# Counting neighbours: two halves of a row packed into one number, one running count over 512 columns instead of 1024

## The chip, the cores and the metric

The kernel runs on one core of a Trainium2 chip. The metric is the device time in microseconds (us) of one execution. Engines are named as in the profile: PE is TensorE (matmul), PEld its weight loads, DVE is VectorE, ACT is ScalarE, POOL is GpSimd, SP the engine whose queue issues most DMAs.

## The reference, cut to what matters

Four graph layers over 16 graphs of 1024 nodes with 64 features. The change touches the first layer, which drops some edges and then takes quantiles over the neighbours that are left:

```python
neigh = (adj_ > 0) & ~eye
ni = neigh.astype(jnp.int32)
rank = jnp.cumsum(ni, axis=-1) - ni          # neighbours left of this column
nb = ni.sum(-1)
skip = jnp.where(nb > T, (nb + K - 1) // K, 1)
rem = neigh & (sk > 1) & (rank % sk == sk - 1) & mask[:, :, None]
rem = rem | jnp.swapaxes(rem, 1, 2)
adj_d = jnp.where(rem, 0.0, adj_)
vals = jnp.where(adj_d[..., None] > 0, x[:, None, :, :], jnp.inf)
s = jnp.sort(vals, axis=2)                   # three quantiles of it, per node and feature
```

The kernel needs the running count along each row of 1024 columns, for 16 x 1024 rows. An edge is in about 6% of the places.

## The kernel before, in words

Graphs are handled in eight pairs. For each pair there are four pieces of work.

- **Sort** (`sort_begin`, `sort_pair`): the 2 x 64 feature columns of a pair are sorted over the nodes, on DVE. A forward pass of 55 compare steps (lines 772 to 776) writes which pairs swapped to DRAM (`m_d`, in groups of four steps). A backward pass (lines 804 to 814) reads those back and turns them into a code per node (`code`), which is transposed (lines 848 to 854), stored to `y_d`, and read by `weights`. At three steps of the forward pass the part that the sort gives up is checked: `tensor_reduce` (line 780) writes `rest_`, a tile with two buffers, and line 784 takes the maximum of the column `past` and `rest_`.
- **Neighbours** (`neighbours`, lines 859 to 958): for each of two graphs, in two halves of four row tiles. A row tile `a` of the adjacency is loaded, `ni` becomes its 0/1 form in 8 bits (line 874), GpSimd clears the diagonal (line 875), and a scan on DVE counts along 1024 columns (line 879, `cum`, 16-bit floats). PE transposes `a` through the two PSUM banks of the pool `nbp` (tile `pk`). Then small operations on four columns (`sk`, lines 894 to 904) find the skip of each row, three ACT passes over `cum` mark the removed edges (`rem`, lines 908 to 910), and PE and ACT build `ndT`, the matrix that is left.
- **Select** (`weights`, `select`, `compact`): the quantiles, by matmuls of `ndT` with `wt` (lines 975 and 1097) and bit work on DVE. `compact` (lines 1227 to 1300) ends with the 56 matmuls of line 1288; it too raises `past` (line 1253).
- **Extras and layers** (`extras`, `layers`): nodes that need a second look, then the rest of the four layers, with the rows `adjT` read from DRAM. The attention of the last layer runs lines 1564 to 1579 for each row tile; line 1586 is the last sum before the output is stored.

`past` is a column of "did any shortcut fail" marks. Where it ends above zero, a general version of the kernel runs at the end. It is one buffer in place, so its updates run in the order in which the program states them.

The order in the program is this: select of pair `p`, extras and layers of pair `p`, then `prepare(p + 1)` (the neighbours of the next pair), then `sort_pair(p + 1)`, then `sort_begin(p + 2)`. A scheduler orders the instructions of each engine from that when the program is built, by readiness and priority, and keeps every data dependency of the stated order. The order on each engine is then fixed; each engine runs its instructions in it. For the first pair the sort is stated before the neighbours.

```python
made = prepare(pr + 1, nb, nbp)
sort_pair(pr + 1, cur, sop)
...
rest_ = so.tile([P, 1], F32, name="rest_", bufs=2)
nc.vector.tensor_reduce(rest_, ...)
nc.vector.tensor_max(past, past, rest_)
```

Of the kernel before, what the change touches and what calls it, by code (L numbers as in the profile page):

```python
# [9 lines left out]
F32 = mybir.dt.float32  # L10
BF16 = mybir.dt.bfloat16
I32 = mybir.dt.int32
U8 = mybir.dt.uint8
U16 = mybir.dt.uint16
I16 = mybir.dt.int16
F16 = mybir.dt.float16
F8 = mybir.dt.float8e5
AF = mybir.ActivationFunctionType
ALU = mybir.AluOpType
AX = mybir.AxisListType  # L20
# [3 lines left out]
P = 128  # L24
# [18 lines left out]
def gnn_stack(ctx, tc, x, adj, nodemask, w, out):  # L43
# [10 lines left out]
    nc = tc.nc  # L54
    B, N, C = x.shape
# [4 lines left out]
    const = ctx.enter_context(tc.tile_pool(name="const", bufs=1))  # L60
    dram = ctx.enter_context(tc.tile_pool(name="dram", bufs=1, space=DRAM))

    ident = const.tile([P, P], F32, name="ident")
    make_identity(nc, ident)
    ident_b = const.tile([P, P], BF16, name="ident_b")
# [83 lines left out]
    past = const.tile([P, 1], F32, name="past")  # L149
# [21 lines left out]
    with tc.tile_pool(name="io", bufs=1, side="right") as io:  # L171
        at0 = io.tile([P, P], I32, name="at0")
        nc.gpsimd.iota(at0, pattern=[[1, P]], base=0, channel_multiplier=0)
        nc.vector.tensor_copy(count, at0)
        at1 = io.tile([P, P], I32, name="at1")
        nc.gpsimd.iota(at1, pattern=[[1, P]], base=0, channel_multiplier=-1)
        nc.vector.tensor_single_scalar(below, at1, 0, op=ALU.is_gt)
    minus_b = const.tile([P, P], BF16, name="minus_b")
    nc.vector.tensor_scalar_mul(minus_b, ident, -1.0)
    taus = const.tile([P, NT, 3], F32, name="taus")  # L180
# [678 lines left out]
    def neighbours(b, ndT, row10, qb, qz, nb, nbp):  # L859

        mask = maskf[:, b * NT : (b + 1) * NT]
        HT = NT // 2
        dq, coef = row10[:, :, :3], row10[:, :, 3:9].rearrange("p t (k s) -> p t k s", s=2)
        pad = 32
        wide = nb.tile([P, NT, pad + N], F8, name="ni")
        nc.gpsimd.memset(wide[:, :, pad - 1 : pad], 0.0)
        ni = wide[:, :, pad:]
        rem = nb.tile([P, NT, N], F8, name="rem")
        for t0 in range(0, NT, HT):
            cum = nb.tile([P, HT, N], F16, name="cum")  # L870
            for t in range(t0, t0 + HT):
                a = nb.tile([P, N], F32, name="a", bufs=2)
                nc.sync.dma_start(a, adj[b, t * P : (t + 1) * P, :])
                nc.vector.tensor_single_scalar(ni[:, t, :], a, 0.0, op=ALU.is_gt, saturate=False)
                nc.gpsimd.tensor_mul(  # L875
                    ni[:, t, t * P : (t + 1) * P], ni[:, t, t * P : (t + 1) * P], offdiag, saturate=False
                )

                nc.vector.tensor_tensor_scan(  # L879
                    cum[:, t - t0, :], ni[:, t, :], wide[:, t, pad - 1 : pad - 1 + N], 0.0, op0=ALU.add, op1=ALU.add  # L880
                )
                for q in range(0, NT, 4):
                    pt = nbp.tile([P, 4, P], F32, name="pk")
                    for k in range(4):
                        nc.tensor.transpose(pt[:, k, :], a[:, (q + k) * P : (q + k + 1) * P], ident)  # L885
                    at = nb.tile([P, 4, P], F32, name="at", bufs=3)
                    nc.scalar.copy(at, pt)  # L887
                    nc.scalar.dma_start(
                        a_d[b % 4, q : q + 4, :, t * P : (t + 1) * P].rearrange("j p n -> p j n"), at
                    )  # L890


            sk = nb.tile([P, 4, HT], F32, name="sk")
            nc.vector.tensor_tensor(sk[:, 2, :], cum[:, :, N - 1], ni[:, t0 : t0 + HT, N - 1], op=ALU.add)
            nbi = nb.tile([P, HT], I32, name="nbi")
            nc.vector.tensor_scalar_add(nbi, sk[:, 2, :], 2.0)
            nc.vector.tensor_single_scalar(nbi, nbi, 2, op=ALU.logical_shift_right)
            nc.vector.tensor_single_scalar(sk[:, 0, :], sk[:, 2, :], 2 * MAX_DEGREE, op=ALU.is_gt)
            nc.vector.tensor_mul(sk[:, 0, :], sk[:, 0, :], mask[:, t0 : t0 + HT])
            nc.vector.tensor_copy(sk[:, 1, :], nbi)  # L900
            nc.vector.scalar_tensor_tensor(sk[:, 1, :], sk[:, 1, :], 1.0, sk[:, 0, :], op0=ALU.add, op1=ALU.mult)
            nc.vector.tensor_scalar(sk[:, 2, :], sk[:, 1, :], -3.0, 4.0, op0=ALU.mult, op1=ALU.add)
            nc.vector.tensor_scalar_add(sk[:, 1, :], sk[:, 1, :], -1.0)
            nc.vector.scalar_tensor_tensor(sk[:, 3, :], sk[:, 1, :], -1.0, sk[:, 1, :], op0=ALU.mult, op1=ALU.mult)
            for t in range(t0, t0 + HT):
                k = t - t0
                sq = nb.tile([P, N], F32, name="sq")
                nc.scalar.activation(sq, cum[:, k, :], AF.Square, bias=sk[:, 2, k : k + 1], scale=1.0)
                nc.scalar.activation(sq, sq, AF.Square, bias=sk[:, 3, k : k + 1], scale=1.0)
                nc.scalar.activation(rem[:, t, :], sq, AF.Relu, bias=one, scale=-1.0, saturate=False)  # L910


                for blocks, to in (
                    ([(j, t) for j in range(t + 1)], ndT[:, : t + 1, t * P : (t + 1) * P]),
                    ([(t, i) for i in range(t)], ndT[:, t, : t * P].rearrange("p (i n) -> p i n", n=P)),
                ):
                    for n, (j, i) in enumerate(blocks):
                        if n % 4 == 0:
                            pk = nbp.tile([P, 4, P], F32, name="pk")
                        terms = [  # L920
                            (ni[:, i, j * P : (j + 1) * P], ident_b),
                            (rem[:, i, j * P : (j + 1) * P], minus_b),
                            (minus_b, rem[:, j, i * P : (i + 1) * P]),
                        ]
                        if i == j:
                            terms.append((ident_b, ident_b))
                        last = n % 4 == 3 or n == len(blocks) - 1
                        for m, (lhs, rhs) in enumerate(terms):
                            nc.tensor.matmul(  # L929
                                pk[:, n % 4, :], lhs, rhs, start=(n % 4 == 0 and m == 0),  # L930
                                stop=(m == len(terms) - 1 and last),
                            )
                        if last:
                            n0, m = n - n % 4, n % 4 + 1
                            nc.scalar.activation(to[:, n0 : n + 1, :], pk[:, :m, :], AF.Relu, saturate=False)  # L935
        pn = nbp.tile([P, 4, P], F32, name="pk")[:, 0, :NT]
        for i in range(NT):
            for j in range(NT):
                nc.tensor.matmul(
                    pn[:, i : i + 1], ndT[:, j, i * P : (i + 1) * P], ones_b[:, 0:1],  # L940
                    start=(i == 0 and j == 0), stop=(i == NT - 1 and j == NT - 1),
                )
        nc.gpsimd.tensor_copy(row10[:, :, 9], ids)

        last = nb.tile([P, NT], F32, name="last")
        nc.vector.tensor_scalar_add(last, pn, -1.0)
        lasts = last.rearrange("p (t o) -> p t o", o=1).to_broadcast([P, NT, 3])
        fr = nb.tile([P, 2, NT, 3], F32, name="fr")
        fi = nb.tile([P, NT, 3], I32, name="fi")
        nc.vector.tensor_mul(fr[:, 0], lasts, taus)  # L950
        nc.vector.tensor_scalar_add(fi, fr[:, 0], -0.4)
        nc.vector.tensor_copy(fr[:, 1], fi)
        nc.vector.tensor_sub(dq, lasts, fr[:, 1])
        nc.vector.tensor_scalar(qb, dq, -2048.0, -2048.0, op0=ALU.mult, op1=ALU.add)
        nc.vector.tensor_scalar(qz, dq[:, :, 0], -1.0, 1.0, op0=ALU.mult, op1=ALU.add)
        nc.vector.tensor_sub(fr[:, 0], fr[:, 0], fr[:, 1])
        nc.vector.tensor_mul(coef[:, :, :, 1], fr[:, 0], shares)
        nc.vector.tensor_sub(coef[:, :, :, 0], shares, coef[:, :, :, 1])
# [663 lines left out]
    for pr in range(pairs):  # L1622
# [17 lines left out]
        with ExitStack() as beside:  # L1640
# [5 lines left out]
            else:  # L1646
                nb_, nbp_ = side_pools()
                nb, nbp = beside.enter_context(nb_), beside.enter_context(nbp_)
# [69 lines left out]
```

## Time and profile before

| What | Value |
|---|---|
| runs, median of 3 | 5790.94 us (5787.52 to 5797.8) |
| the profiled execution | 5786.15 us, its span 5784.4 us |
| DVE busy | 5034.9 us, 87% of the span |
| PE busy | 4378.1 us, 76% |
| ACT busy | 3789.4 us, 66% |
| scans of 1024 columns, 128 of them | 292.4 us, 2285 ns each |
| chain that ended last, by engine | PE 40%, DVE 24%, ACT 23%, DMA 9%, issue 3% |

Busy time is the time in which an engine worked; where several engines take turns, no engine is busy all the time, and the time is set by the chain of work that passes from one to the other. The kernel has eight periods. In the trace a period is cut at two events: the first `wt` of a pair (line 975), and the last matmul of line 1288. From the first to the second is called the select stage here, from the second to the first `wt` of the next pair the side stage.

### The profile page before, as it was taken

To read this page: it belongs to the slowest core of one execution; us is meant where nothing else is said; L and a number is where in the kernel's file an instruction comes from. 1 tells how busy PE (TensorE), PEld (TensorE's weight loads), DVE (VectorE), ACT (ScalarE), POOL (GpSimd) and SP (SyncE) were. 2 spreads that over 40 slices of the span, in tenths; PEclk is the share of its full clock that TensorE was granted. 3 is DMA by queue.
4 is the path that set the end of the run, shared out by engine and by line. 5 is a ranking of instruction groups with operands and counts; after the bars stand their busy time and mean duration, and the time that the engine had idled before them with its cause. 6 is when DMAs were issued, how large, how long until landed. Compare 5 with 4: busy or idle time off the path is not lost.

```text
span 5784.4 us, 114212 instructions
## 1 busy us (share of the span) xinstructions
PE 4378.1 (76%) x45010; PEld 2731.3 (47%) x45010; DVE 5034.9 (87%) x13175; ACT 3789.4 (66%) x5739; POOL 169.8 (3%) x292
## 2 busy tenths in 40 slices
PE   1488677896878958788588885788767886779956
PEld 1355443554435544455434554355543554535642
DVE  9899888998889987999879998899888998888755
ACT  2587657775586855867558666686657866477835
POOL 3000000000000000000000000000000000000000
PEclk5699878997789977899688996899878997789967
DMA  3401264013631047210562115611255012630030
GB/s 128 127 23 45 86 205 133 29 38 113 220 96 35 28 133 237 62 40 23 166 211 55 41 53 167 203 32 40 82 175 172 26 40 90 215 110 18 10 100 5
DMA packets 519811, 551.45 MB, mean 95 GB/s; under 512 B 263296, under 2 KB 413056, under 8 KB 519264
## 3 DMA queue, kind: packets, MB, share of 16 engines
q1 hardware_dynamic: 376864, 459.65, 25.5%
q10 hardware_dynamic: 140064, 81.84, 4.6%
q8 instruction: 355, 5.82, 0.4%
q0 software_dynamic: 2336, 2.57, 0.2%
q14 instruction: 192, 1.57, 0.1%
HBM read 360.17 MB, written 183.76 MB: 94 GB/s over the span
## 4 chain that ended last, share of the span: by engine, by line
PE 40%; DVE 24%; ACT 23%; DMA 9%; issue 3%; POOL 0%; SPq 0%; ACTq 0%; DVEq 0%; POOLq 0%
PE comb L1097 13%; ACT sign L1152 8%; PE cand L1197 6%; PE bank L1462 5%; DVE y L1168 4%; PE comb L1288 3%; ACT y L1105 3%; DMA adjT<-a_d 2%; DVE cum L879 2%; DMA a_d<-at 2%; DVE wt L975 2%; DVE cand L1205 2%; PE pk L929 2%; ACT nat L1128 1%; PE bank L1446 1%
## 5 line engine op out<-in xcount | busy, mean ns | idle before, releaser
L1097 PE MATMUL comb<-wt,ndT 128*128 128x512 fp8e5 x6144 | 1439.2, 386 | 144.4 <-ACT sign L1152 111.8
L1105 ACT ACTIVATE y<-comb,qb 128x512 int16<-128x512 f32 x1152 | 743.4, 712 | 505.3 <-PE comb L1097 504.2
L1097 PEld LDWEIGHTS <-ndT 128*128 128x128 fp8e5 x6144 | 591.1, 99 | 864.7 <-issue 231.6
L1152 ACT ACTIVATE sign<-comb,lower 128x1024 fp8e5<-128x1024 int16 (+1 forms) x640 | 694.5, 1085 | 0.0
L1152 ACT ACTIVATE sign<-comb,half 128x1024 fp8e5<-128x1024 int16 (+1 forms) x640 | 689.1, 1077 | 0.0
L1197 PE MATMUL cand<-vtab,sign 128*128 128x48 f16 (+1 forms) x18432 | 663.1, 191 | 23.1 <-DVE agg L1074 16.2
L1168 DVE TENSOR_TENSOR y<-y 128x512 uint16<-128x512 uint16 (+5 forms) x896 | 669.4, 789 | 10.8 <-PE comb L1150 10.0
L1197 PEld LDWEIGHTS <-sign 128*128 128x128 fp8e5 x18432 | 637.6, 96 | 82.0 <-issue 21.2
L1205 DVE COPY_PREDICATED cand<-w_f,cand 128x256 f32<-128x256 uint16 (+1 forms) x1536 | 531.9, 378 | 86.1 <-PE cand L1197 83.7
L887 ACT COPY at<-pk 128x512 f32<-128x512 f32 x256 | 147.3, 586 | 372.7 <-PE pk L885 199.8
L1150 PE MATMUL comb<-ident_b,y 128*128 128x128 bf16 x4608 | 307.2, 218 | 101.9 <-ACT sign L1152 70.8
L929 PE MATMUL pk<-minus_b,rem 128*128 128x128 bf16 x1024 | 231.9, 251 | 178.8 <-ACT rem L910 178.8
L1150 PEld LDWEIGHTS <-y 128*128 128x128 bf16 x4608 | 284.9, 97 | 127.1 <-issue 126.9
L929 PE MATMUL pk<-ident_b,ni 128*128 128x128 bf16 x1024 | 229.1, 247 | 110.4 <-ACT ndT L935 60.7
L879 DVE TENSOR_TENSOR_SCAN cum<-ni 128x1024 f16<-128x1024 fp8e5 x128 | 292.4, 2285 | 15.5 <-POOL ni L875 15.5
L885 PE MATMUL pk<-ident,a 128*128 128x128 f32 x1024 | 192.1, 330 | 149.9 <-DMA a<-in_adj_dram 100.1
L1462 PE MATMUL bank<-att,hs 128*64 128x512 f32 x512 | 191.1, 857 | 122.0 <-ACT hs L1578 122.0
L1462 PE MATMUL bank<-adjT,nd 128*64 128x512 f32 x896 | 256.2, 642 | 29.9 <-DMA adjT<-a_d 29.6
L975 DVE TENSOR_SCALAR wt<-node 128x2048 uint8<-128x2048 f16 x224 | 262.5, 1220 | 18.4 <-PE comb L1288 18.1
L775 DVE TENSOR_TENSOR s<-s 128x512 f32<-128x512 f32 (+1 forms) x440 | 276.0, 627 | 0.0
L776 DVE TENSOR_TENSOR s<-s 128x512 f32<-128x512 f32 (+1 forms) x440 | 275.1, 625 | 0.0
L1163 DVE TENSOR_SCALAR y<-y 128x4608 int16<-128x4608 int16 x128 | 173.5, 1355 | 90.7 <-ACT y L1105 89.3
(381 smaller groups left out, 8355.7 us busy)
## 6 DMA issues: line engine op xcount, KB each, us to landing
adjT<-a_d SPq DMA_DIRECT2D x336, 512.0 KB
a<-in_adj_dram SPq DMA_DIRECT2D x128, 512.0 KB
a_d<-at ACTq DMA_DIRECT2D x256, 256.0 KB
m_d<-swapped SPq DMA_DIRECT2D x104, 512.0 KB
swapped<-m_d SPq DMA_DIRECT2D x104, 512.0 KB
n_d<-nat SPq DMA_DIRECT2D x128, 128.0 KB
x_d<-xr SPq DMA_DIRECT2D x48, 256.0 KB
comb_x<-x_d ACTq DMA_DIRECT2D x24, 512.0 KB
```

Of the source, the lines that this page charges most:

```text
L775: nc.vector.tensor_tensor(to_lo, lo, hi, op=ALU.max)
L879: nc.vector.tensor_tensor_scan(cum[:, t - t0, :], ni[:, t, :], wide[:, t, pad - 1 : pad - 1 + N], 0.0, op0=ALU.add, op1=ALU.add)
L929: nc.tensor.matmul(pk[:, n % 4, :], lhs, rhs, start=(n % 4 == 0 and m == 0), stop=(m == len(terms) - 1 and last),)
L975: nc.vector.tensor_scalar(wt[g][:, :, k : k + 4, :].bitcast(U8), node, 4.0 * (25 + CODE * (8 * g + k)), 4.0 * 26, op0=ALU.add, op1=ALU.min,)
L1097: nc.tensor.matmul(pw, ndT[:, j, t * P : (t + 1) * P], wt[1 + g8][:, j].rearrange("p w c -> p (w c)"), start=(j == 0), stop=(j == NT - 1),)
L1105: nc.scalar.activation(y[:, 0, chunks, at : at + 8 * d_].rearrange("p q (w d) -> p q w d", d=d_), pw.rearrange("p (w q d) -> p q w d", w=8 ...
L1150: nc.tensor.transpose(pt[:, q - q0, :], y[:, 0, q, :].bitcast(BF16), ident_b)
L1152: nc.scalar.activation(signs[tl][s][:, q0:q1, :], pt.bitcast(I16), AF.Sign, bias=before[s], scale=-1.0, saturate=False,)
L1168: nc.vector.tensor_tensor(v[:, :, :, :n], v[:, :, :, :n], v[:, :, :, n : 2 * n], op=ALU.max)
L1197: nc.tensor.matmul(cand[:, e, at : at + 12 * d_].rearrange("p (d l) -> p d l", l=12), signs[tl][sec][:, chunk, :], tab[:, q, :, half_ * 12 ...
L1205: nc.vector.copy_predicated(v[:, :, :, dst : dst + k], mk.to_broadcast([P, 2, C // 2, k]), v[:, :, :, frm : frm + k])
L1462: nc.tensor.matmul(po[to : to + C, :], lhs, rhs[:, f * HALF : (f + 1) * HALF], start=(j == 0), stop=(j == NT - 1))
```

## The change

The scan counts both halves of a row at once. PE adds the left half of `ni` and 65536 times the right half into one PSUM bank of 512 columns (two matmuls, with the identity and `high_b` as weights), and the same right half, shifted by one column, once more (a third matmul). The shift for the left half stays with the scan's second operand. The scan then runs over 512 columns and writes 32-bit integers, which are read back as two 16-bit halves. The totals of the two halves are added, the left total is added to the start value of the right half, and the first of the three ACT passes becomes two passes over 512 columns each. Because the packed number must stay below 2^24 to be exact, the largest last count of each half of the row tiles is checked: `many` is reduced from `cum`, and `past` is raised by it. That is one more update of `past` for each half, four for each pair, stated in `neighbours`.

```diff
+    high_b = const.tile([P, P], BF16, name="high_b")
+    nc.vector.tensor_scalar_mul(high_b, ident, 65536.0)
...
         for t0 in range(0, NT, HT):
-            cum = nb.tile([P, HT, N], F16, name="cum")
+            cum = nb.tile([P, HT, N // 2], I32, name="cum")
+            halves_ = cum.bitcast(U16).rearrange("p t (n f) -> p t n f", f=2)
             for t in range(t0, t0 + HT):
...
+                both_ = nbp.tile([P, 4, P], F32, name="pk").rearrange("p k n -> p (k n)")
+                nc.tensor.matmul(both_, ident_b, ni[:, t, : N // 2], start=True, stop=False)
+                nc.tensor.matmul(both_, high_b, ni[:, t, N // 2 :], start=False, stop=False)
+                nc.tensor.matmul(both_[:, 1:], high_b, ni[:, t, N // 2 : N - 1], start=False, stop=True)
                 nc.vector.tensor_tensor_scan(
-                    cum[:, t - t0, :], ni[:, t, :], wide[:, t, pad - 1 : pad - 1 + N], 0.0, op0=ALU.add, op1=ALU.add
+                    cum[:, t - t0, :], both_, wide[:, t, pad - 1 : pad - 1 + N // 2], 0.0, op0=ALU.add, op1=ALU.add
                 )
...
-            sk = nb.tile([P, 4, HT], F32, name="sk")
-            nc.vector.tensor_tensor(sk[:, 2, :], cum[:, :, N - 1], ni[:, t0 : t0 + HT, N - 1], op=ALU.add)
+            sk = nb.tile([P, 6, HT], F32, name="sk")
+            for f in range(2):
+                nc.vector.tensor_tensor(
+                    sk[:, 4 + f, :], halves_[:, :, N // 2 - 1, f], ni[:, t0 : t0 + HT, (f + 1) * N // 2 - 1], op=ALU.add
+                )
+            nc.vector.tensor_add(sk[:, 2, :], sk[:, 4, :], sk[:, 5, :])
+            many = nb.tile([P, 1], F32, name="many")
+            nc.vector.tensor_reduce(many, cum[:, :, N // 2 - 1], axis=AX.X, op=ALU.max)
+            nc.vector.tensor_scalar_add(many, many, 1.0 - 2.0**24)
+            nc.vector.tensor_max(past, past, many)
...
             nc.vector.tensor_scalar(sk[:, 2, :], sk[:, 1, :], -3.0, 4.0, op0=ALU.mult, op1=ALU.add)
+            nc.vector.tensor_add(sk[:, 4, :], sk[:, 4, :], sk[:, 2, :])
...
-                nc.scalar.activation(sq, cum[:, k, :], AF.Square, bias=sk[:, 2, k : k + 1], scale=1.0)
+                for f in range(2):
+                    nc.scalar.activation(
+                        sq[:, f * N // 2 : (f + 1) * N // 2], halves_[:, k, :, f], AF.Square,
+                        bias=sk[:, 2 + 2 * f, k : k + 1], scale=1.0,
+                    )
```

## The prediction

> **What bounds the kernel now.** I read the engine rows first, then the stretches by stage, then the groups of the side stage, then single events of `past`.
>
> ```profile
> PE 4378.1 (76%) x45010; PEld 2731.3 (47%) x45010; DVE 5034.9 (87%) x13175; ACT 3789.4 (66%) x5739; POOL 169.8 (3%) x292
> ```
>
> DVE is busiest, but 87% is a mean over stages. The stretches, select and side stage of the second and the last period (columns: stretch, length, then busy us and count of PE, PEld, DVE, ACT, POOL, granted clock, DMA share, GB/s):
>
> ```profile
> 281.00:664.00 383.00, 332.66 (x3866) 210.84 (x3865) 361.82 (x912) 279.41 (x455) 3.12 (x4) 0.94 0.11 33
> 664.00:982.00 318.00, 216.47 (x1776) 129.06 (x1775) 265.98 (x731) 195.17 (x267) 12.93 (x24) 0.76 0.59 185
> ...
> 5170.00:5529.00 359.00, 321.65 (x3841) 206.10 (x3840) 275.71 (x740) 277.29 (x451) 2.02 (x2) 0.96 0.07 15
> 5529.00:5784.00 255.00, 150.17 (x1094) 86.27 (x1092) 133.91 (x392) 101.92 (x120) 3.20 (x6) 0.67 0.17 56
> ```
>
> The side stage takes 318 us with a next pair to prepare, and 255 us in the last period, where neither neighbours nor a sort run. So extras and layers alone need about 244 us up to their last attention (5529 to 5773), and 311 us (664 to 975) with the rest between them. DVE works 84% of that stage. What fills it:
>
> ```profile
> L879 DVE TENSOR_TENSOR_SCAN cum<-ni 128x1024 f16<-128x1024 fp8e5 x16 | 36.6, 2286 | 2.1 <-POOL ni L875 2.1
> L814 DVE TENSOR_TENSOR code<-code,xo 128x1024 uint16<-128x1024 uint16 (+1 forms) x33 | 22.2, 672 | 0.4
> L804 DVE TENSOR_TENSOR xo<-code 128x512 uint16<-128x512 uint16 (+1 forms) x54 | 21.9, 405 | 0.7
> ...
> L806 DVE TENSOR_TENSOR xo<-xo,swapped 128x512 uint16<-128x512 uint16 x39 | 16.4, 420 | 2.9 <-DMA swapped<-m_d 2.4
> ```
>
> The scans are only 36.6 us of it. The backward pass of the sort is 84.3 us (these three rows and lines 808, 811, 812 with 6.0, 9.1 and 8.7). It costs little now because it lies in the gaps of extras and layers. That cover is what the change touches, through `past`:
>
> ```profile
> 457.77 0.42 DVE L780 TENSOR_REDUCE rest__10637<-s 128x1 f32<-128x256 f32 x1
> ...
> 638.66 0.16 DVE L1253 TENSOR_TENSOR past<-past,over 128x1 f32<-128x1 f32 x1
> ...
> 644.77 0.15 DVE L784 TENSOR_TENSOR past<-past,rest__10637 128x1 f32<-128x1 f32 x1
> ...
> 645.17 0.41 DVE L780 TENSOR_REDUCE rest__10695<-s 128x1 f32<-128x256 f32 x1
> ```
>
> The sort's first check is computed at 457.77, but its update of `past` waits until 644.77, behind the second `compact` (638.66), which stands earlier in the program. The second check (506.31) takes the other buffer of `rest_`, so the third check (645.17) and all of the sort behind it wait too. Today the wait ends with the select stage.
>
> **The change, part by part.**
>
> *The scan.* The scan of 8 columns (line 1242) has a median of 174 ns, that of 1024 has 2285, so a column costs (2285 - 174) / 1016 = 2.08 ns and 512 columns 174 + 504 x 2.08 = 1.22 us: 1.06 us less, 128 times, 136 us of DVE (17 us in each of eight pairs). Its first input now comes from PSUM. The nearest rows are two sums of 128x512, line 1488 from PSUM and line 1489 from SBUF: 691 ns each, so I take nothing for that.
>
> Against that row stands the Trainium skill, Perfetto Trace Analysis, section Optimizing Scalar/DVE Operations: an access costs VectorE about 60 ns on SBUF and about 125 ns on PSUM. By that page, as an estimate, the 128 scans would give back 8 us.
>
> *Small operations.* Each half gains seven operations on four columns or one and loses one; the removed one (line 894) takes 157 ns. 32 x 6 x 0.16 = 31 us busy at most, 4 us a pair.
>
> *ACT.* Two Squares of 512 replace one of 1024 (1146 ns). Nearest rows: copies of 128x512, 586 ns (line 887), and 712 ns in line 1105. 128 x (2 x 0.59 - 1.15) = 4 us, at most 35 us by the dearer row; ACT has room (66%). Nothing on the path.
>
> *PE.* 3 x 128 matmuls of 512 columns. Line 1097 runs eight such in 1.9 us when the clock is full, 0.24 us each, mean 386 ns: 92 to 148 us, 12 to 18 in a side stage where PE idles a third of the time. The new wait is a ring: DVE (`ni`), POOL, PE (pack), DVE (scan). Queued behind the pack on PE are the eight transposes of the same row tile, and the pack holds one of the two `pk` banks until the scan has read it. In the built order other DVE work stands between `ni` and its scan. I take it as covered and leave it in the range of the stage.
>
> *The hold.* `neighbours` of the next pair is stated before `sort_pair` of that pair, and now updates `past` four times. By the mechanism just shown the sort's third check must wait for the fourth of these. I compared the order of DVE's instructions in the two built programs, which is fixed. Of the 187 operations of a backward pass, in each of the seven later sorts all 187 stand ahead of the last sum of the layers before the change. After it, one does (an early read of `code`). Rows of the changed order in the second period:
>
> ```
> 1787 last two attention products (old line 1573)
> 1789 past<-past,many              the fourth
> 1793 past<-past,rest__10855       the sort's first check
> 1798 rest__10913                  its third check
> 1801 sort goes on (25 forward operations left)
> 1811 last sum of the layers (old line 1586)
> 1831 backward pass begins, 186 operations
> 2049 first wt of the next pair
> ```
>
> So DVE does the rest of the sort when extras, layers and neighbours are done, and the next select waits, since `wt` needs the code. The tail from the last attention to the first `wt`: 25 forward operations 15 us (lines 772, 775, 776: 5.5 + 4.4 + 5.1 in this stage); from the last forward operation through the store and reload of `swapped` to line 806 5 us (147.9 to 152.8 in the first stage); the backward pass 84 us busy, 90 us with the gaps of a dependent chain (a step of 0.44 + 0.43 + 0.70 takes 1.65, 261.99 to 263.64); differences and quantile constants that stand between 6 us. `last` stands early in the backward pass and needs the whole end of the neighbours on ACT and PE. That took 24 to 28 us after `sk` was ready (754.88 to 778.62, 148.97 to 176.48), and only about 20 us of DVE work stand between: 5 us. SP's queue now has the 24 `vtab` loads, up to 10 in a row at 0.6 to 0.9 us each, between the reloads of `swapped`, of which one serves 6.6 us of steps: 5 us. From the last backward operation to `wt`, 11 us:
>
> ```profile
> 270.42 1.06 ACT s L848
> ...
> 275.08 2.94 DMA y_d<-s
> 278.04 2.59 DMA node<-y_d
> ...
> 281.38 13.73 DVE wt L975 x12
> ```
>
> Sum 15 + 5 + 90 + 6 + 5 + 5 + 11 = 137; I take 135, where some 7 us are there now (975 to 982). Bounds: 120 if the waits hide each other, 150 if they don't.
>
> What comes back: without the sort the stage up to the last attention is shorter than 311 us, but not below the 244 us of the last period. The surplus of 67 us comes from 132 us more of DVE work, and also from 66 us more of PE and 93 us more of ACT, which stay. The sort (104 us) and the scans (14 net) are most of DVE's surplus. Between half and four fifths of the 67 us gone gives 278 to 258: I take 268.
>
> The side stage becomes 268 + 135 = 403 us for 318: 85 us more, 7 times, 595 us. The select stage keeps its part of the forward pass (146 operations before and after) and its time. In the first stage the sort is stated first, and DVE is busy 92% of the time: it gains 16 x 1.06 less 4, 13 us. Sum: 5786.15 + 595 - 13 = 6368 us for the profiled execution, which lies 5 us below the median of the runs: 6370 us (rounded).
>
> **The rivals.**
>
> *VectorE gets its time back (faster).* If the held sort had other work to hide it, the scans' saving counts: 136 - 31 = 105 us, 5680 us if all of it lies on the path. The chain gives line 879 2%, 120 us, so it could. It decides if DVE stays the bound through the whole stage, that is if extras and layers run 85 us a stage faster without the sort, 183 us where the last period needs 244. That row speaks against it. 4%.
>
> *The stage doesn't shrink.* Extras and layers are held by PE and ACT, not by DVE: 311 + 150 - 318 = 143 us a stage, 6775 us; with a tail of 135 6670. PE's 216 us at a clock of 0.76 and the new ring on two banks speak for it, DVE's 84% against. 20%.
>
> *The stage shrinks to its chain and the waits of the tail hide.* 244 + 120 - 318 = 46 us, 6100 us. For it: in the last period the same work takes 244. Against: neighbours still run beside it. 18%.
>
> *It doesn't do what it says:* if a packed count reached 2^24, the general version would run as well. That takes 128 neighbours in half a row, where about 31 are there. 1%.
>
> **How the numbers follow.** The forecast, 57%, spans 258 to 285 us and a tail of 125 to 145: 6250 to 6550. Taking in half of each slow and quick rival gives 6170 to 6600. A difference of 0.2% (12 us) is about what a measurement of this kernel can tell from none. Slower has 57 + 20 + 18 = 95%, with the general version 96%, less 1 for cases between; same 1%; faster 4%.
>
> **What would show it.** Right: the windows show DVE alone at work for over 100 us at the end of each side stage, PE and ACT nearly idle; lines 804 to 814 of the old numbering lie after the last attention; the `past` updates of the sort's first check come over 400 us after the check; the scan is near 1.22 us. Wrong: scans over 1.5 us, a tail under 100 us, or a side stage whose first part stays at 311 us. I am wrong altogether if the backward pass finds other DVE work beside it.

## The result and the profile after

| | before | after |
|---|---|---|
| median of the runs | 5789.23 us (4 runs) | 6456.40 us (4 runs, 6439.38 to 6464.85) |
| ratio | | 1.1152, 95% interval 1.1133 to 1.1172 |
| the profiled execution | 5786.15 us, span 5784.4 us | 6439.38 us, span 6437.6 us |

The change makes the kernel 11.5% slower; the forecast was 6370 us, within 6170 to 6600. The engine rows of the changed kernel:

```profile
PE 4461.7 (69%) x45394; PEld 2776.4 (43%) x45394; DVE 5039.8 (78%) x13368; ACT 3830.2 (59%) x5867; POOL 159.7 (2%) x292
```

No engine does much more work than before (TensorE 84 us more, ScalarE 41, VectorE 5), and every share of the span is lower: the added time is waiting. The stretches of the second period show where (select, the side stage up to the last attention, and the tail up to the next `wt`; then 50 us out of that tail; columns as before the change):

```profile
275.00:653.00 378.00, 328.93 (x3867) 209.86 (x3866) 353.36 (x890) 279.36 (x456) 2.96 (x4) 0.96 0.11 32
653.00:944.00 291.00, 208.49 (x1580) 121.94 (x1580) 165.69 (x496) 168.02 (x224) 11.96 (x24) 0.76 0.52 163
944.00:1070.00 126.00, 22.59 (x230) 17.01 (x226) 106.70 (x276) 30.32 (x54) 0.00 (x0) 0.54 0.32 91
...
1000.00:1050.00 50.00, 0.00 (x0) 0.00 (x0) 46.77 (x108) 0.00 (x0) 0.00 (x0) 0.50 0.33 95
```

In the tail VectorE does most of the work; for the 50 us of the last line TensorE and ScalarE execute nothing. Up to the last attention VectorE has only 166 us of work in 291 us, so it first has too little and then too much. The timeline shows the cause at `past` (line 782 computes a check of the sort, 786 raises `past` by it, 909 is the new update):

```profile
448.70 0.41 DVE L782 TENSOR_REDUCE rest__10855<-s 128x1 f32<-128x256 f32 x1
...
942.77 0.14 DVE L909 TENSOR_TENSOR past<-past,many 128x1 f32<-128x1 f32 x1
...
943.03 0.15 DVE L786 TENSOR_TENSOR past<-past,rest__10855 128x1 f32<-128x1 f32 x1
...
943.24 0.15 DVE L786 TENSOR_TENSOR past<-past,rest__10881 128x1 f32<-128x1 f32 x1
...
943.38 0.41 DVE L782 TENSOR_REDUCE rest__10913<-s 128x1 f32<-128x256 f32 x1
```

The first check waits 494 us for its update, from 448.70 to 943.03; before the change it waited 187 us (457.77 to 644.77). The third check, which needs one of the two buffers of `rest_`, follows 0.14 us after the second update, and the rest of the sort comes behind it. Who waits for the sort is seen in the page's groups, with the idle time in the last columns:

```profile
L855 PE MATMUL ps<-ident,s 128*128 128x128 f32 x64 | 16.9, 416 | 620.7 <-ACT s L850 615.5
...
L850 ACT ACTIVATE s<-code 128x1024 f32<-128x1024 uint16 x8 | 8.4, 1055 | 565.4 <-DVE code L814 565.4
```

ScalarE is idle for 565 us until the code of a pair is ready, and TensorE for 616 us behind ScalarE. The new work itself, in the groups by line (busy us, mean ns, then idle time before it):

```profile
L925 ACT ACTIVATE sq<-cum,sk 128x512 f32<-128x512 uint16 x256 | 177.2, 716 | 50.8 <-DVE sk L917 45.5 <-DVE sk L918 2.9
L886 DVE TENSOR_TENSOR_SCAN cum<-pk,ni 128x512 int32<-128x512 f32 x128 | 156.0, 1219 | 50.8 <-PE pk L885 49.9 <-POOL ni L878 0.3
...
L883 PE MATMUL pk<-ni,ident_b 128*128 128x512 fp8e5 x128 | 59.3, 463 | 124.7 <-POOL ni L878 87.2 <-ACT ndT L955 23.0 <-DVE ni L877 12.6
```

The scan is as short as forecast, 1219 ns for 2285 ns. TensorE waits 87 us for GpSimd in front of the packs, and the scans wait 50 us for TensorE.

### The profile page after: what moved, and what is told of

The parts are those of the page before. It is cut to its first block, busy times and chain, and to the rows that moved or that the text cites. A ratio compares the mean times of both kernels' runs of the same rounds, so it can differ in the third digit from the quotient of the medians.

```text
span 6437.6 us, 115379 instructions
## 1 busy us (share of the span) xinstructions
PE 4461.7 (69%) x45394; PEld 2776.4 (43%) x45394; DVE 5039.8 (78%) x13368; ACT 3830.2 (59%) x5867; POOL 159.7 (2%) x292
## 4 chain that ended last, share of the span: by engine, by line
PE 37%; DVE 31%; ACT 20%; DMA 7%; issue 4%; POOL 0%; ACTq 0%; SPq 0%; DVEq 0%; POOLq 0%
PE comb L1117 11%; ACT sign L1172 7%; PE cand L1217 6%; PE bank L1482 4%; DVE y L1188 4%; PE comb L1308 3%; DMA adjT<-a_d 3%; ACT y L1125 2%; DVE xo L806 2%; DVE code L816 2%; DVE xo L808 2%; PE pk L949 2%; DVE wt L995 2%; DVE cand L1225 1%; DMA a<-in_adj_dram 1%
## 5 line engine op out<-in xcount | busy, mean ns | idle before, releaser
L855 PE MATMUL ps<-ident,s 128*128 128x128 f32 x64 | 16.9, 416 | 620.7 <-ACT s L850 615.5
L949 PE MATMUL pk<-minus_b,rem 128*128 128x128 bf16 x1024 | 250.5, 267 | 183.1 <-ACT rem L930 183.1
L949 PE MATMUL pk<-ident_b,ni 128*128 128x128 bf16 x1024 | 250.3, 261 | 60.1 <-ACT ndT L955 39.1
L1482 PE MATMUL bank<-adjT,nd 128*64 128x512 f32 x896 | 238.9, 635 | 40.2 <-DMA adjT<-a_d 39.9
```

Source lines behind the costliest of these rows:

```text
L949: nc.tensor.matmul(pk[:, n % 4, :], lhs, rhs, start=(n % 4 == 0 and m == 0), stop=(m == len(terms) - 1 and last),)
L1482: nc.tensor.matmul(po[to : to + C, :], lhs, rhs[:, f * HALF : (f + 1) * HALF], start=(j == 0), stop=(j == NT - 1))
```

## The experiments

Two theories were put against each other. **The hold:** the update of `past` by `many`, with the two buffers of `rest_`, makes the whole loss, and the packing itself is harmless or a gain. **The packing:** the new matmuls, the wait for them, or ScalarE's split passes make it.

All kernels are read by the same events. Times are us. Select, the part of the side stage up to the last attention, and the tail (from there to the next first `wt`; negative where `wt` comes first) are means over the seven periods that prepare a next pair. The last column is the place of `last`, the end of the neighbours, against the last attention, the mean of the first six of these.

| kernel | median | ratio, 95% interval | span | select | to last attention | tail | `last` |
|---|---|---|---|---|---|---|---|
| before | 5789 | | 5784.4 | 382.9 | 313.2 | 0.3 | -13 |
| after | 6456 | 1.1133 to 1.1172 | 6437.6 | 379.1 | 285.5 | 127.0 | +28 |
| 1 no update | 5803 | 1.0020 to 1.0061 | 5782.4 | 379.1 | 297.8 | 20.6 | +13 |
| 2 own column | 5824 | 1.0042 to 1.0087 | 5828.4 | 381.8 | 302.6 | 19.2 | +14 |
| 3 update alone | 6287 | 1.0853 to 1.0902 | 6269.3 | 379.6 | 298.5 | 88.8 | -12 |
| 4 four `rest_` | 5816 | 1.0031 to 1.0061 | 5815.0 | 386.9 | 298.2 | 17.2 | +11 |
| 5 pack first | 5859 | 1.0115 to 1.0151 | 5855.6 | 381.5 | 307.1 | 18.7 | +13 |
| 6 transposes first | 5846 | 1.0091 to 1.0126 | 5843.5 | 382.3 | 309.1 | 15.4 | +10 |
| 7 one Square | 5830 | 1.0059 to 1.0097 | 5826.5 | 379.9 | 304.3 | 19.5 | +10 |
| 8 before, two columns | 5748 | 0.9914 to 0.9955 | 5746.3 | 392.2 | 310.1 | -12.7 | -30 |
| 9 three columns | 5825 | 1.0047 to 1.0088 | 5831.9 | 388.4 | 293.0 | 21.7 | +17 |

### What makes the loss: runs 1 to 4

**Run 1, the changed kernel without the update.** `many` is computed, but `past` isn't raised by it.

```diff
-            nc.vector.tensor_max(past, past, many)
```

> The changed kernel without the one update of `past` in `neighbours` (so the overflow check of the packed count has no effect; everything else, the reduction of `many` too, is kept). Theory H, the hold: the sort is free again, in the built order all 187 backward operations stand ahead of the last sum of the layers; the 127 us tail of each side stage is gone and the stage is back at 318 us or less. 5789 us less what the scans save: at most 105 us (128 x 1.06 - 31), at least nothing; I expect 5720, range 5680 to 5800. Rival R, the ring of VectorE, GpSimd and TensorE and the shared PSUM banks: the update is only three small instructions, 6400 to 6460 us stay.

5803.47 us: taking out four operations of 0.15 us in each pair takes away 653 us of the added 667. The tail falls from 127 to 21 us. It stays a little slower than before, and 3 us above the range that was expected; the expected gain is missing.

**Run 2, the same check in a column of its own.** Nothing is left out.

```diff
-            nc.vector.tensor_max(past, past, many)
+            nc.vector.tensor_max(past_n, past_n, many)
...
+        nc.vector.tensor_max(past, past, past_n)
```

> The changed kernel with the neighbours' updates in a column of their own, `past_n`, joined to `past` once at the end: nothing is left out. Theory H: the sort no longer waits, so the same as without the update, 5680 to 5800 us, and within 20 us of that run. If it is faster than the kernel before, the packed scan was worth it and only the flag was in the wrong place. Rival R: 6400 to 6460 us.

5824.38 us, 21 us above run 1. The shared column held the sort, not the operations on it. Again no gain, and 24 us above the range that was expected.

**Run 3, the update alone in the kernel before.** The scan over 1024 columns and ScalarE's one pass stay; no pack.

```diff
             sk = nb.tile([P, 4, HT], F32, name="sk")
+            many = nb.tile([P, 1], F32, name="many")
+            nc.vector.tensor_reduce(many, cum[:, :, N - 1], axis=AX.X, op=ALU.max)
+            nc.vector.tensor_scalar_add(many, many, 1.0 - 2.0**24)
+            nc.vector.tensor_max(past, past, many)
```

> The kernel before, with its scan of 1024 columns, and only the reduction of `many` and the update of `past` added to `neighbours`. Theory H: the hold alone makes the loss. In the built order 155 of 187 backward operations stand behind the last sum of the layers, so the tail is about 70 to 115 us (155 of 187 of the pass, 70 us, 11 us to `wt`, and up to 30 us of the rest of the forward pass, some of which now lies beside the layers); seven times 60 to 110 us less what the shorter stage gives back: 6200 to 6500 us. Rival R: the packing is what costs, so 5790 to 5800 us here.

6287.01 us, within what the hold expected: the loss needs no packing. The timeline and the stretch of its tail (`past` by `many` is line 898 here, by the check 784):

```profile
878.89 0.15 DVE L898 TENSOR_TENSOR past<-past,many 128x1 f32<-128x1 f32 x1
...
879.08 0.16 DVE L784 TENSOR_TENSOR past<-past,rest__10669 128x1 f32<-128x1 f32 x1
```

```profile
960.00:1048.00 88.00, 5.46 (x18) 2.15 (x16) 76.54 (x207) 6.49 (x11) 0.00 (x0) 0.52 0.32 81
```

The same picture: the check waits for the fourth `many`, then VectorE works nearly alone. The hold ends earlier, at 879 instead of 943, and in the built order 32 of the 187 backward operations still stand ahead of the last sum of the layers, for one in the changed kernel. So its tail is 89 us, 38 less, and its side part 13 us longer; seven times 25 is 175 us, about the 169 us between the two medians.

**Run 4, the changed kernel with four buffers of `rest_`.** The updates of `past` stay as they are.

```diff
-                    rest_ = so.tile([P, 1], F32, name="rest_", bufs=2)
+                    rest_ = so.tile([P, 1], F32, name="rest_", bufs=4)
```

> The changed kernel with four buffers for `rest_` in place of two; `past` is still updated by the neighbours. Theory H in its exact form (the wait goes through the buffers of `rest_`): the three checks no longer block the forward pass; the next thing that waits for `past` is the sort's last update, which holds the sorted tile `srt`, one of three buffers, so the transposition of the code may still wait for the neighbours but the backward pass doesn't. In the built order all 187 operations stand ahead of the last sum of the layers. 5700 to 5850 us, 0 to 15 us a period above the run with the column of its own. If it were any dependence on `past` rather than the buffers, 6400 to 6460 us would stay.

5815.53 us, within the expected range. The checks' updates still wait (the first until 912.9), but each check has its own buffer: the third check of the second pair now comes at 540.4 instead of 943.4. Runs 1, 2 and 4 take away all but 16 to 37 us of the loss, at three places of one chain, and run 3 makes 500 us of it without the packing. The hold is shown.

### Why the packing, once free, gains nothing: runs 5 to 7

VectorE got its time: its busy time in run 2 is 4943.4 us, 91.5 less than before. The side part up to the last attention is 11 us shorter. But a tail of 19 us follows, which is no sort: in the first side stage of run 2 the code was ready 35 us ahead of the last attention. `last` shows what it is, first in run 2, then in the kernel before (timelines; line 968 and line 946):

```profile
980.10 0.17 DVE L968 TENSOR_SCALAR last<-pk 128x8 f32<-128x8 f32 x1 [6.55 <-PE pk L961]
```

```profile
961.79 0.16 DVE L946 TENSOR_SCALAR last<-pk 128x8 f32<-128x8 f32 x1
```

In run 2 VectorE is idle for 6.55 us, waiting for the neighbours' last matmuls, and `wt` follows at 986.03. Before, `last` came 13 us ahead of the last attention and waited for nothing. The neighbours now end last in that stage, but only just. The code, stored to `y_d` at 960.94, is loaded again for `wt` only at 980.40, in SP's queue behind transfers of the sort after it, and is back at 983.4; the first operation that needs it runs at 984.83. So an earlier `last`, with nothing else moved, could win 1.4 us of this tail. In run 1 the last wait of VectorE ahead of `wt` is for the store of that code (0.7 us), in run 7 for its reload (1.9 us). No run was made for this second chain alone.

The stretch from 915 to 980 us, first before, then run 2:

```profile
915.00:980.00 65.00, 45.97 (x295) 20.96 (x294) 54.11 (x181) 51.54 (x73) 0.00 (x0) 0.74 0.39 106
```

```profile
915.00:980.00 65.00, 42.67 (x318) 23.02 (x317) 40.76 (x138) 56.74 (x81) 0.00 (x0) 0.78 0.33 82
```

VectorE works 13 us less there, and that time is idle (6.55 us of it is the wait for `last`); ScalarE works 5 us more, 87% of the stretch. The groups of run 2 show the new ring (line 885 is the first matmul of the pack, 894 the transposes):

```profile
L894 PE MATMUL pk<-ident,a 128*128 128x128 f32 x1024 | 195.1, 313 | 69.2 <-DVE cum L888 40.1 <-ACT at L896 28.2
...
L885 PE MATMUL pk<-ni,ident_b 128*128 128x512 fp8e5 x128 | 55.8, 436 | 144.7 <-POOL ni L880 109.0 <-DVE ni L879 23.1 <-ACT at L896 8.6
```

TensorE waits 145 us ahead of the packs, and its transposes 40 us for the scan that reads the pack's bank. Three parts of that were tried one at a time, on run 2.

**Run 5, pack and scan placed early** in the orders of TensorE and VectorE.

```diff
+                with tc.high_priority():
-                both_ = nbp.tile([P, 4, P], F32, name="pk").rearrange("p k n -> p (k n)")
+                    both_ = nbp.tile([P, 4, P], F32, name="pk").rearrange("p k n -> p (k n)")
...
-                nc.vector.tensor_tensor_scan(
+                    nc.vector.tensor_tensor_scan(
...
```

> The second run (own column) with the three pack matmuls and the scan of each row tile given high priority, so that the scheduler puts them early in the order of TensorE and VectorE. In the second run's first side stage the end of the neighbours (the tile `last`) comes 322 us after the select stage's end, where it came 297 us after it in the kernel before, and the last scans of a pair wait 15 to 40 us between GpSimd's diagonal and their pack. Theory of the late neighbours: that wait is a place in TensorE's order; with it gone `last` comes back to about 300 us, the tail falls from 20 to under 10 us, and the time from 5824 to 5680 to 5760 us. Rival, ScalarE's two dearer Squares make the neighbours late: 5800 to 5830. Rival, the stage is full on all engines together: the layers wait instead, 5800 to 5850.

5859.31 us, above all three ranges. The last scan of the second pair starts 239 us after the select stage's end instead of 261 (206 in the kernel before), and the last `sk` is ready at 245.5 instead of 269.5. But ScalarE's last `rem` of the pair ends at 313.8, where run 2 had 317.4 and the kernel before 250.5, and `last` ends at 319.9 instead of 322.5. So of 24 us won at `sk`, 4 are left after ScalarE's passes; the theory of the late pack, in this form, is refuted.

**Run 6, the transposes stated ahead of the pack.**

```diff
-                both_ = nbp.tile([P, 4, P], F32, name="pk").rearrange("p k n -> p (k n)")
...
-                nc.vector.tensor_tensor_scan(
...
                 for q in range(0, NT, 4):
                     pt = nbp.tile([P, 4, P], F32, name="pk")
...
+                both_ = nbp.tile([P, 4, P], F32, name="pk").rearrange("p k n -> p (k n)")
...
+                nc.vector.tensor_tensor_scan(
...
```

> The second run (own column) with the eight transposes of a row tile stated ahead of its pack, so that they no longer queue behind a pack that waits for GpSimd. Theory of the late neighbours: the transposes' wait only costs a little of `a`'s two buffers; 0 to 6 us a stage, 5780 to 5825 us. Rival, the ring of the two `pk` banks is what holds: transposes that run early free `a` and the banks, the tail under 10 us and 5700 to 5760.

5845.74 us, above both. The tail is 4 us shorter and the part ahead of it 6.5 us longer. The transposes still wait 33 us for scans (40 in run 2), and 56 us for ScalarE's copies of them (28 in run 2). Both banks stay shared; a bank more was not tried.

**Run 7, one Square over 1024 columns** with one start value.

```diff
-                for f in range(2):
-                    nc.scalar.activation(
-                        sq[:, f * N // 2 : (f + 1) * N // 2], halves_[:, k, :, f], AF.Square,
-                        bias=sk[:, 2 + 2 * f, k : k + 1], scale=1.0,
-                    )
+                nc.scalar.activation(
+                    sq.rearrange("p (f n) -> p f n", f=2), halves_[:, k].rearrange("p n f -> p f n"), AF.Square,
+                    bias=sk[:, 2, k : k + 1], scale=1.0,
+                )
```

> The second run (own column) with one Square over 1024 columns instead of two over 512; the left half's total is left out of the right half's start value, so other edges are marked. Theory of the late neighbours by TensorE's order: ScalarE's 28 us more are 3.5 us a stage, not all of them on the path; 5800 to 5825 us, tail 15 to 20. Rival, ScalarE's Squares make the neighbours late: tail under 10 us, 5720 to 5770.

5830.41 us, as run 2: 5 us above the first range, and 60 above the rival's. The group of that line:

```profile
L926 ACT ACTIVATE sq<-cum,sk 128x1024 f32<-128x1024 uint16 x128 | 146.6, 1145 | 38.3 <-DVE sk L919 36.3
```

That gives ScalarE its 28 us back, and the end doesn't move. The run changes more than the pass: its built order also puts the code 5 us behind the last attention, where run 2 had it 35 us ahead, so that code and `last` now come close together.

### Columns and places: runs 8 and 9, and three with a different priority

**Run 8, the kernel before with `compact` in a column of its own.** Its updates hold the sort through the same two buffers, until the select stage ends.

```diff
-        nc.vector.tensor_max(past, past, over)
+        nc.vector.tensor_max(past_c, past_c, over)
...
+        nc.vector.tensor_max(past, past, past_c)
```

> The kernel before with `compact` raising a column of its own, joined at the end, so that the sort no longer waits for `compact` in the select stage. Theory of the hold: the third check comes earlier than the select stage's end, but VectorE is 94% busy there, so the sort's work displaces select's and little is won: 5760 to 5810 us. Rival, the hold by `compact` costs what the hold by `many` costs in kind: the side stage shortens by 10 us or more each, 5650 to 5740.

5748.03 us, ratio 0.9935 (0.9914 to 0.9955): the fastest kernel of this study, between the two expectations. Its timeline:

```profile
548.26 0.41 DVE L782 TENSOR_REDUCE rest__10697<-s 128x1 f32<-128x256 f32 x1
...
548.78 0.15 DVE L786 TENSOR_TENSOR past<-past,rest__10697 128x1 f32<-128x1 f32 x1
...
950.51 0.17 DVE L948 TENSOR_SCALAR last<-pk 128x8 f32<-128x8 f32 x1 [0.52 <-PE pk L941]
```

The third check comes 97 us earlier than before (645.17). The backward pass begins at 646 instead of 715, `last` stands 30 us ahead of the last attention, and the first `wt` 13 us ahead of it. The select stage pays 9 us for the sort work that it takes in, and the side stage with its tail gives 16: some 7 us a period.

**Run 9, the packed count with both columns apart.**

```diff
-            nc.vector.tensor_max(past, past, many)
+            nc.vector.tensor_max(past_n, past_n, many)
...
-        nc.vector.tensor_max(past, past, over)
+        nc.vector.tensor_max(past_c, past_c, over)
```

> The packed count with columns of their own for the neighbours and for `compact`, joined at the end: neither holds the sort. The kernel before won 40 us by the second of these columns alone. Theory (the packing by itself costs the 35 us of the second run, because the neighbours end late): 5770 to 5800 us, tail near 20 us. Rival (the sort and the packing compete for the same time of VectorE, so that with the sort earlier the packing pays): 5680 to 5740 us.

5825.01 us, above both expectations and 77 us above run 8, which is the same without the packing (their ratios to the kernel before, 1.0068 and 0.9935, have intervals far apart). Up to the last attention it takes 17 us less than run 8, but `wt` comes 34 us later against that point, and `last` stands 17 us behind it instead of 30 ahead. An earlier sort doesn't help: the code of the second pair is ready 22 us ahead of the last attention, and VectorE then waits 6.1 us for `last`.

**Runs 10 to 12: all of the neighbours at high priority** in the side stage, in run 2, in run 8, and in run 9.

```diff
                 if pr + 1 < pairs:
-                    made = prepare(pr + 1, nb, nbp)
+                    with tc.high_priority():
+                        made = prepare(pr + 1, nb, nbp)
```

> The second run (own column) with the whole of the next pair's neighbours at high priority in the side stage. Theory of the late neighbours: in the second run the stage ended with `last`, 14 us after the last attention, because TensorE's and ScalarE's part of the neighbours stands behind the layers in their orders; now `last` comes before 300 us after the select stage's end. If the neighbours alone were late, the tail falls under 8 us with the part up to the last attention at 300 to 308: 5720 to 5790 us. Rival, the stage is full on TensorE and ScalarE together, so that the layers become late by what the neighbours win: the part up to the last attention 315 to 325, 5790 to 5860 us.

> The kernel before with `compact`'s own column and the next pair's neighbours at high priority: the control of the next run, with the scan over 1024 columns. Theory (neighbours were not late there, `last` came 13 us before the last attention): no gain over the kernel with the column alone, 5740 to 5790 us. Rival (early neighbours free the end of the stage): 5680 to 5735 us.

> The packed count with the two columns of their own and the next pair's neighbours at high priority. Theory (the packing loses by late neighbours only): below its control, the same without the packing, by up to 60 us: 5670 to 5740 us. Rival (TensorE's and ScalarE's added work and the wait for the pack cost what VectorE saves): the same as its control or up to 40 us above it, 5740 to 5820 us.

5997.41, 5949.73 and 6076.10 us, all above every expectation. In run 10 `last` comes 206 us after the select stage's end, so the neighbours are early indeed; but in that first side stage the extras end at 171 us (118 in run 2), and the last attention comes at 362 us (308 in run 2). What the neighbours win, extras and layers lose more than once over. These runs overshoot, and don't price a small shift.

What is shown: in every packed kernel of the table `last` stands 10 to 28 us behind the last attention, in every kernel with the old scan 12 to 30 us ahead of it. What stays open: which part of the packing makes the neighbours late, and how much of the tail would go if they were not, as the reload of the code ends close behind them. An early pack and scan hardly move `last`. The transposes behind the pack, and ScalarE's second pass, move it by some 4 us when taken alone, no more than runs 1, 2 and 4 differ among themselves (+11 to +14), and neither makes the kernel faster.

## Why the prediction was right, and which terms were off

**The hold, right.** The named chain is what the timeline and runs 1 to 4 show: the fourth `many`, the sort's first updates, two buffers of `rest_`, the third check, and all of the sort behind. Of the signs that were named for it, two came in full: the update more than 400 us after its check, the scan near 1.22 us. The third came in part: in the second period's tail of 127 us VectorE is busy for 110, but alone at work for 83, not over 100; TensorE and ScalarE are both idle for 91.

**The tail, right: 127.0 us for 135.** In the second period the forward rest and the reload took 21.9 us (942.8, the last attention, to 964.7; forecast 15 + 5), the backward pass 93.3 (to 1058.0), and the way from there to `wt` 12.3 (forecast 11). The backward pass with its three extras was put at 90 + 6 + 5 + 5. Most of these 16 us hid: `last` came at 971, early in the backward pass. The tail of the kernel before was read too long: 7 us (975 to 982), where the first `wt` starts at 976.7, 1.8 us after the last attention. So the tail grew by 126.7 us for 128 in the forecast, and that near agreement is two errors that cancel.

**The side stage without its sort, mis-sized.** It became 285.5 us, where 268 was forecast with bounds of 258 and 285. Only 28 of the 67 us above the last period's 244 went, not half to four fifths of them. From 750 to 800 us TensorE was busy for 47.2 of 50 us and VectorE for 15.4, and from 800 to 850 us TensorE for 43.3 with the DMA engines at 0.89: there the stage ran on TensorE and the rows `adjT`, not on VectorE. The rival that said so was right in part. The 244 us were also no measure of the same work: in the last period the layers read their rows from 16 held tiles, loaded once, and have four PSUM banks each, while every earlier side stage issues 48 loads of `adjT` (512 KB each) through three buffers, with three banks and two. The DMA share of that last stage is 0.17, for 0.52 in the changed kernel's side stage. How much of the missed gain this makes, no run separates.

**The balance.** By the same events, the part up to the last attention fell by 27.7 us, where the forecast took 43: 15 us, 107 us over seven stages. Against that the tail is 9 us less in all than forecast, the select stages 33 us less (they were taken as unchanged). The first stage gained 6.5 us for 13. 582 us were forecast; 582 + 107 - 9 - 33 + 6.5 = 653.5, and the spans differ by 653.2. So that the time lies within 90 us of the forecast is partly luck: 42 of the 107 us were taken back by terms that came out smaller than taken. By the prediction's own sum, its bounds of stage and tail give 6233 to 6562 us, not 6250 to 6550; the result lies in both.

**The rival that VectorE gets its time back** was given 4%, on the condition that the sort finds cover. Runs 1, 2, 4 and 9 give it that cover. VectorE's busy time falls by 91.5 us in run 2, where 105 were worked out, and the time does not fall. (In the changed kernel itself the busy time does not fall, since it counts overlapping operations once and they overlap less there; the sum of the operations' times falls alike, from 6007 us to 5914, and to 5912 in run 2.) So the rival's price, 5680 us, was wrong as well as its chance small: it counted a gain of the busiest engine as time, where the neighbours' chain over GpSimd, TensorE and ScalarE, and the reload of the code close behind it, now end last.

**The small terms.** The scan from PSUM took 1219 ns, and 1.22 us came from rows that read SBUF. The Trainium skill, Perfetto Trace Analysis, section Optimizing Scalar/DVE Operations, would, as an estimate from its figures, add 65 ns; the scan's row in the profile doesn't show that, though the types of input and output changed as well. TensorE's pack was put at 92 to 148 us in all and kept TensorE busy for 141 (129 in run 2): the mean record of a matmul is longer, 436 to 469 ns, but the records overlap. The ring was put at nothing, and TensorE waits 125 us ahead of the packs. ScalarE's half Square was taken from a copy of 586 ns and took 716; the dearer bound, 712 ns, was the right row, as it too is an activation with a column as bias. The Trainium skill, ScalarE: Activation LUTs, section What ACT_TABLE_LOAD costs, gives for that form about 280 ns and 0.833 ns a column, as an estimate 707 and 1133 ns; the runs show 716 and 1145, and agree within 10 and 12 ns.

## What to carry to other kernels

An in-place mark that several parts raise is a dependency between them, in the order in which the program states them. Before adding an update to it, find who updates it next and what small buffers sit behind that one; give each part its own column and join them at the end, or give every pending value a buffer. An engine's saved time counts only if the chain that ends the stage runs on that engine: look at which of the parallel chains ends last, and by how much the next one trails it, before a step is put behind one more engine, as the scan was here behind TensorE.

## What the runs showed of the hardware

- Reading 16-bit halves with a stride of two costs ScalarE nothing visible: 1145 ns for 1024 columns out of 32-bit words, 1147 ns for the same pass over a plain 16-bit row. Splitting the pass in two costs 286 ns (2 x 715.5 - 1145).
- A matmul's record is no constant price. The pack's 384 matmuls of 512 columns (8-bit moving operand) in the changed kernel fall into two kinds: 253 records of up to 400 ns (median of all 379 to 389 by line) and 104 of 600 ns or more. Around 16 of the short ones the granted clock was 0.97 to 1.00; around 11 of 13 of the long ones it was 0.50. Short ones start 0.21 us apart (725.27, 725.49, 725.70), long ones 0.42 (739.52, 739.94, 740.37). The means of 451 to 469 ns mix the two; among the 6144 matmuls of that size in the select stage (line 1117, mean 385) only 142 are long.
